# Layer 1 of a two-layer graph attention kernel: transposes in two separate halves, each beside a held piece of the projection

## The chip, the cores and the metric

The kernel runs on one core of a Trainium2 chip. The metric is the time of one execution on the device in microseconds. Three runs of the kernel before gave 1902.05, 1904.1 and 1896.26; the median is 1902.05 us. The profile is of one further execution.

The engines are named as in the profile: PE is TensorE (PEld are its weight loads), DVE is VectorE, ACT is ScalarE, POOL is GpSimd, SP is SyncE, whose queue here only issues DMAs.

## The reference

`x` has 3327 rows of 1024 numbers, `adj` is a 3327 x 3327 matrix of zeros and ones with about 0.5% ones and a full diagonal. There are two layers, each a graph attention with a residual and a layer norm. Layer 0 has 8 heads of 128, layer 1 has one head of 1024 and a relu:

```
# layer 0
h = x @ W0; e = leaky_relu(alpha_src[:, None] + alpha_dst[None, :])   # per head
x1 = layer_norm(x + softmax(where(adj == 0, -inf, e)) @ h)
# layer 1
h = x1 @ W1; e = leaky_relu(h @ a1 + (h @ a2).T)
out = layer_norm(x1 + relu(softmax(where(adj > 0, e, -9e15)) @ h))
```

## The kernel before, in words

Rows are worked on in 26 tiles of 128. A first stage (to about 480 us) projects `x`, scans `adj` into lists of neighbours, and decides between a dense and a sparse way; these inputs take the sparse one, `sparse`, L743. It runs layer 0 over all tiles and then layer 1 over all tiles, both by the function `pipeline` (L1058). The order in which instructions are issued is written out by hand (L1101, a manual schedule): what Python calls first stands first in each engine's queue, and each engine takes its queue in that order.

In layer 1 the attention sum is formed on the rows before the projection: the kernel sums the rows of layer 0's output `y_d`, divides, and projects the sum by `W1` afterwards (`wt1`). One tile of the class `Target` (L960) goes through these methods:

- `prepare` (L966) transposes the row scores to R on PE (L969) and takes their exp on ACT into the PSUM bank `way` (L971); it makes the one-hot marks on DVE (L833, L837) and loads the tile's own rows of `y_d` on SP's queue (L976). It is called for tile t+1 in block 2 of tile t.
- `fetch` (L988) gathers neighbours' rows by indirect DMAs of POOL (L817), four for each of blocks 0 to 3 and one for block 4, into a ring of five buffers, one tile ahead.
- `weights` (L994) makes the attention weights `es` of one block on DVE (L1001, L1002, L1004), through `way`.
- `sums` (L1007) adds a block into three accumulators on PE (L1013). Blocks 0 to 3 use four groups of 32 columns at a time; block 4 uses the full width.
- `close` (L1018) divides the sums and adds the tile's own row, giving `z` (DVE L1021 to L1023, ACT L1027, DVE L1030).
- `finish` (L1035) is a generator of ten steps. Steps 1 and 2 each transpose half of `z` on PE into the one bank of tag T (L176) and empty it on ACT into `xT` (L179). Steps 3 to 6 are the projection's first half of columns, two of eight `k` a step (L1045), with the relu and residual of that half on DVE at the end (L1048); steps 7 to 10 are the second half.
- `settle` (L1053) is the layer norm of the result and the store to `out`: DVE L192 to L194, ACT's square root L195, then after a yield DVE L197 and L199 and the DMA L1056. It is put on the queue `ahead` when the tenth step is done.

`pipeline` runs a tile's five blocks. In block 0 it closes the tile before; after each block's sums it runs steps of finished tiles from a queue `work`, and one step of `ahead`. For layer 1 the numbers are one step ahead of block 0's sums and then 2, 2, 2, 2 and 1 after the blocks' sums. So tile t has in block 0 the last step of tile t-2's projection, then its sums, then both transposes of tile t-1; after sums 1 to 3 four `k` of the projection of t-1 each, and after sums 4 two more.

ACT has to load a table ahead of the square root and another ahead of the exp of R; both loads stand in its queue in every tile of layer 1.

PSUM has eight banks. `sparse` gives five to the accumulators (tag A), one to the projection and to layer 0's denominators (S), one to transposes (T), one to `way` (E). In layer 1 a tile takes three of tag A.

The buffers of tag `z` (three) hold `z` and the output `o` in turn; `ys` (three, by t mod 3) holds the tiles' own rows.

Of the kernel before, what the change touches and what calls it, by code (L numbers as in the profile page):

```python
# [19 lines left out]
P = 128  # L20
# [6 lines left out]
def kernel(  # L27
# [31 lines left out]
    NT = (N + P - 1) // P  # L59
# [11 lines left out]
    EB = 4  # L71
# [5 lines left out]
    CUTS = (0, 342, 684, D + 1)  # L77
# [79 lines left out]
    class Phase:  # L157
# [7 lines left out]
        def bank(self, tag, shape, name, dt=F32):  # L165
            return self.psum.tile(shape, dt, tag=tag, name=name, bufs=self.banks[tag])
# [286 lines left out]
    with ExitStack() as own, tc.manual_schedule():  # L453
        ph = Phase(own, "proj", {"A": 2, "S": 1, "T": 2})
        pool, bank = ph.pool, ph.bank
# [205 lines left out]
        for t in range(3, NT):  # L661
# [3 lines left out]
            if t == 12:  # L665
                n, own = NT - 1, pool.tile([P, NT], I32, bufs=1, name="own")
# [27 lines left out]
        tr = bank("T", [1, P], "trc")  # L694
# [46 lines left out]


    def sparse(own):  # L743
        ph = Phase(own, "sparse", {"A": 5, "S": 1, "T": 1, "E": 1})
        pool, bank, sbuf = ph.pool, ph.bank, ph.sbuf
        NS = 5
        srcs = [pool.tile([P, NG, HG], F32, bufs=1, name=f"src{n}") for n in range(NS)]
# [8 lines left out]
        way = bank("E", [P, HALF], "way")  # L756
# [24 lines left out]
        def score_weights():  # L781
            for n, a in enumerate((a1_src, a1_dst)):
                av = sbuf("z", [P, D], 3, "av")
                spread(av, a)
                for k in range(KT):
                    pr = sbuf("pr", [P, D], 1)
                    nc.vector.scalar_tensor_tensor(
                        pr, wt1[:, k, :], 1.0, av, op0=OP.mult, op1=OP.mult, accum_out=wc[:, n, k : k + 1]
                    )
                    if k % 3 == 2:  # L790
                        yield
                for g in range(2):
                    tr = bank("T", [P, 4, P], "tr")
                    for k in range(4):
                        nc.tensor.transpose(
                            tr[:, k, :], wc[:, n, 4 * g + k : 4 * g + k + 1].to_broadcast([P, P]), ident
                        )
                    nc.scalar.activation(wa[n][:, g * HALF : (g + 1) * HALF], tr.rearrange("p a b -> p (a b)"), AF.Copy)
                yield

        def run(work, steps=1):

            while work and steps:
                try:
                    next(work[0])
                    steps -= 1
                except StopIteration:
                    work.popleft()

        ahead = deque([score_weights()])  # L810
# [17 lines left out]
        def marks(t):  # L828

            m = NB - 1  # L830
            oh = sbuf("oh", [P, m * GT + P], 2)
            parts = oh[:, : m * GT].rearrange("p (b t) -> p b t", t=GT), oh[:, m * GT :]
            nc.vector.tensor_tensor(  # L833
                parts[0], io_t[:, :GT].unsqueeze(1).to_broadcast([P, m, GT]),
                tgt[:, t, :m].unsqueeze(2).to_broadcast([P, m, GT]), OP.is_equal,
            )
            nc.vector.tensor_scalar(parts[1], io_t, tgt[:, t, m:], None, op0=OP.is_equal)  # L837
            return parts

        class Layer0:  # L840
# [5 lines left out]
            def prepare(self):  # L846
                self.re = listed.pop(self.t)
                self.oh, self.oh2 = marks(self.t)
                self.y = ys[self.t % 3]
                load_rows(self.y[:, :D], x, self.t)  # L850
                self.h = sbuf("own", [P, HW0], 2)
                nc.sync.dma_start(self.h, h0_d[self.t * P : (self.t + 1) * P, :])
# [13 lines left out]
            def begin(self):  # L866
                self.acc = [bank("A", [P, 4, DH], "acc") for _ in range(2)]
# [92 lines left out]
        class Target:  # L960
# [4 lines left out]

            def prepare(self):  # L966
                t = self.t
                tr = bank("T", [P, P], "tr")
                nc.tensor.transpose(tr, r1.s[:, t, :].to_broadcast([P, P]), ident)  # L969
                self.r = way[:, (t % 2) * P : (t % 2 + 1) * P].rearrange("p (g t) -> p g t", g=NG)  # L970
                nc.scalar.activation(  # L971
                    self.r.rearrange("p g t -> p (g t)"), tr, AF.Exp, scale=1 - SLOPE
                )
                self.oh, self.oh2 = marks(t)
                self.res = ys[t % 3]
                nc.sync.dma_start(self.res, y_d[t * P : (t + 1) * P, :])  # L976
# [12 lines left out]
                self.src[b] = gather(y_d, HW, self.t, b)  # L989

            def begin(self):
                self.acc = [bank("A", [P, CUTS[1]], "acc1") for _ in range(3)]

            def weights(self, b):  # L994
                s = self.src[b]
# [59 lines left out]
                for r in pieces(self.t):  # L1055
                    nc.sync.dma_start(out[at(self.t, r), :], o[r])  # L1056

        def pipeline(kind, late, behind, get):  # L1058

            tiles = [kind(t) for t in range(NT)]
            work = deque()
            get(0)
            tiles[0].prepare()
            for b in range(EB + 1):
                tiles[0].fetch(b)
            tiles[0].weights(0)
            for t, tg in enumerate(tiles):  # L1070
                tg.begin()
                for b in range(EB + 1):
                    if b == 0 and t:
                        tiles[t - 1].close()
                        run(work, late)
                    if b == 0 and t + 1 < NT:
                        get(t + 1)
                    if b == 2 and t + 1 < NT:
                        tiles[t + 1].prepare()
                    if b == 0:  # L1080
                        tg.own()
                    if b < EB:
                        tg.weights(b + 1)
                    elif t + 1 < NT:
                        tiles[t + 1].weights(0)
                    tg.sums(b)
                    if t + 1 < NT:
                        tiles[t + 1].fetch(b)
                    run(work, behind[b])
                    if t or b:  # L1090
                        run(ahead)
                if t == 0 and late:
                    work.append(iter(range(1)))
                work.append(tg.finish())
            tiles[-1].close()
            run(work, late)
            run(ahead, -1)
            run(work, -1)
            run(ahead, -1)

        with tc.manual_schedule():  # L1101
            pipeline(Layer0, 0, (1, 1, 1, 1, 1), get_edges)
            pipeline(Target, 1, (2, 2, 2, 2, 1), lambda t: None)


    def by_pairs(own):
# [119 lines left out]
    with arm.Else():  # L1226
        with ExitStack() as own:
            sparse(own)
# [23 lines left out]
```

## Time and profile before

| | |
|---|---|
| median of three runs | 1902.05 us (1896.26 to 1904.1) |
| profiled execution | 1954.92 us, span 1953.2 us, mean granted clock 0.907 |
| PE busy | 1668.2 us, 85% of the span |
| DVE, ACT, POOL busy | 1151.9, 546.6, 1039.7 us |
| first stage, layer 0, layer 1 | to about 480 us, to about 1215 us, from about 1240 us |
| sums of layer 1 (L1013) on PE | 265.1 us |
| projection of layer 1 (L1045) on PE | 382.3 us, 832 matmuls of 603 ns |
| transposes of z (L176), of R (L969), from 1210 us on | 35.2 us, 7.2 us |
| gathers of layer 1 (L817) on POOL | 416 into the ring, 1002 ns each, and 26 for block 4 |

How to read the views: a group's line names engine, line, operation, output and inputs, then the number of instructions, their busy time, and the idle time of the engine ahead of them with what ended it. The view of waits has for each waiter and releaser the total, the number and the longest. The timeline has the start, the time covered, and in brackets the engine's idle time before. "issue" means that the profile shows nothing that was waited for. In the slices each digit is a fortieth of the span, in tenths.

### The profile page before, as it was taken

The page shows a single profiled execution, that of the slowest core. Times are in us where ns is not written, and L with a number is a line of the kernel's source. Part 1 is how long each engine was busy: PE and PEld are TensorE (multiplying, and loading weights), DVE is VectorE, ACT ScalarE, POOL GpSimd, SP SyncE. Part 2 cuts the span into 40 slices and gives each one's busy share as a digit, 9 for nine tenths or more (in the row PEclk, how much of TensorE's full clock was granted, in tenths as well). Part 3 has the DMA queues.
Part 4 walks back from the last instruction along what each step waited for, and adds up shares of the span by engine and source line. Part 5 has one row for each costly group of instructions (what it writes and reads, how often), then busy time and mean ns, then how long its engine had stood idle before and what let it go on. Part 6 is the DMA issues. An engine that isn't in the chain of part 4 may idle for free.

```text
span 1953.2 us, 36865 instructions
## 1 busy us (share of the span) xinstructions
PE 1668.2 (85%) x14091; PEld 915.1 (47%) x14091; DVE 1151.9 (59%) x3087; ACT 546.6 (28%) x1422; POOL 1039.7 (53%) x1391
## 2 busy tenths in 40 slices
PE   8799999997577787777877777479999999999997
PEld 5456555564444554544454445134444444444343
DVE  6699989985575566556665566134444444444442
ACT  5445554442122222222222222012122222222221
POOL 4322222211666666666666663566666666666650
PEclk9899999998677887879787887589999999999999
DMA  7556554311999999999999996899999999999980
GB/s 183 95 129 130 112 94 92 88 60 64 404 356 377 370 365 387 381 372 363 379 377 375 369 371 225 335 318 386 378 378 367 381 366 373 357 377 368 355 340 32
DMA packets 171063, 567.68 MB, mean 291 GB/s; under 512 B 27690, under 2 KB 34346, under 8 KB 170878
## 3 DMA queue, kind: packets, MB, share of 16 engines
q0 software_dynamic: 131056, 455.68, 67.3%
q1 hardware_dynamic: 39822, 109.56, 15.1%
q8 instruction: 113, 1.85, 0.4%
q14 instruction: 72, 0.59, 0.1%
HBM read 578.85 MB, written 42.97 MB: 318 GB/s over the span
## 4 chain that ended last, share of the span: by engine, by line
PE 74%; issue 10%; DVE 6%; ACT 5%; DMA 2%; another core or an unknown queue 1%; POOL 1%; SPq 0%; POOLq 0%; DVEq 0%; ACTq 0%
PE mm L1045 19%; PE acc L914 19%; PE acc L1013 13%; PE mm L479 12%; PE acc L906 4%; PE acc L896 3%; ACT junk L311 3%; PE tr L176 2%; DMA wt<-in_L_gnn_W_dram 1%; DMA src<-h_d,idx 1%; PE den L922 1%; PE xp L411 1%; DVE top L274 1%; PE den L935 1%
## 5 line engine op out<-in xcount | busy, mean ns | idle before, releaser
L817 POOL DMA_INDIRECT src<-h_d,idx x416 | 448.9, 1079 | 228.0 <-PE acc L914 83.1
L817 POOL DMA_INDIRECT src<-y_d,idx x416 | 416.8, 1002 | 250.9 <-issue 84.4
L914 PE MATMUL acc<-src,e 128*32 128x128 f32 x6656 | 396.2, 321 | 167.0 <-issue 138.1
L914 PEld LDWEIGHTS acc<-src,e 128*32 128x32 f32 x6656 | 254.1, 127 | 332.5 <-issue 309.4
L479 PE MATMUL mm<-wt,xT 128*128 128x347 f32 (+1 forms) x1248 | 402.0, 468 | 3.0 <-DMA wt<-in_L_gnn_W_dram 2.6
L1045 PE MATMUL mm<-wt,xT 128*128 128x512 f32 x832 | 382.3, 603 | 3.1 <-DVE o L1048 3.1
L479 PEld LDWEIGHTS mm<-wt,xT 128*128 128x128 f32 x1248 | 228.2, 192 | 105.5 <-issue 4.0
L1013 PE MATMUL acc<-src,es 128*32 128x342 f32 (+1 forms) x2496 | 215.9, 467 | 39.2 <-DVE es L1004 24.9
L1045 PEld LDWEIGHTS mm<-wt,xT 128*128 128x128 f32 x832 | 151.9, 190 | 201.6 <-issue 184.9
L884 DVE TENSOR_TENSOR e<-oh,way 128x1024 f32<-128x1024 f32 x130 | 158.7, 1221 | 110.0 <-ACT w L882 29.5
L1013 PEld LDWEIGHTS acc<-src,es 128*32 128x32 f32 x2496 | 73.6, 112 | 171.5 <-issue 163.4
L882 ACT ACTIVATE w<-way 128x32 f32<-128x32 f32 x130 | 25.0, 193 | 449.1 <-PE acc L914 177.2
L1027 ACT ACTIVATE z<-y,ri 128x342 f32<-128x342 f32 (+1 forms) x78 | 39.5, 569 | 290.5 <-issue 118.7
L1001 DVE TENSOR_TENSOR way<-way,src 128x128 f32<-128x128 f32 x104 | 31.1, 299 | 147.2 <-ACT way L971 57.1
L1048 DVE SCALAR_TENSOR_TENSOR o<-mm,y 128x512 f32<-128x512 f32 x52 | 35.9, 691 | 108.9 <-PE mm L1045 73.9
L179 ACT ACTIVATE xT<-tr 128x512 f32<-128x512 f32 x104 | 59.4, 596 | 128.0 <-PE tr L176 115.0
L906 PE MATMUL acc<-own,ident 128*128 128x512 f32 x104 | 81.0, 871 | 0.0
L311 ACT ACTIVATE junk<-ad 128x3328 uint8<-128x3328 uint8 x26 | 78.4, 3014 | 2.5 <-POOL ad L308 2.5
L1021 DVE TENSOR_TENSOR ri<-acc,es 128x1 f32<-128x1 f32 x26 | 4.1, 158 | 124.3 <-PE acc L1013 116.7
L938 DVE TENSOR_TENSOR ri<-den,es 128x8 f32<-128x8 f32 x26 | 4.3, 166 | 119.8 <-PE den L935 119.8
L296 POOL CAST mvs<-r 128x8 bf16<-128x8 f32 x26 | 6.1, 235 | 122.8 <-ACT r L295 122.8
L864 ACT ACTIVATE own<-own,es 128x128 f32<-128x128 f32 x208 | 63.6, 388 | 26.2 <-DVE es L861 16.0
(194 smaller groups left out, 2020.8 us busy)
## 6 DMA issues: line engine op xcount, KB each, us to landing
h_d<-ht SPq DMA_DIRECT2D x26, 520.0 KB
own<-h_d SPq DMA_DIRECT2D x26, 520.0 KB
y_d<-y SPq DMA_DIRECT2D x26, 514.0 KB
y<-y_d SPq DMA_DIRECT2D x26, 514.0 KB
x<-in_x_dram SPq DMA_DIRECT2D x25, 512.0 KB
y<-in_x_dram SPq DMA_DIRECT2D x25, 512.0 KB
out_dram<-o SPq DMA_DIRECT2D x25, 512.0 KB
ad<-in_adj_dram POOLq DMA_DIRECT2D x25, 415.9 KB
```

The lines of the kernel that those rows point to most:

```text
L179: nc.scalar.activation(part, tr, AF.Copy)
L311: nc.scalar.activation(junk, ad, AF.Copy, accum_out=self.deg)
L479: nc.tensor.matmul(acc, xT[t][:, k, :], wt[:, k, CUTS0[c] : CUTS0[c + 1]], start=k == 0, stop=k == KT - 1)
L817: nc.gpsimd.indirect_dma_start(out=s[:, g, :w], out_offset=None, in_=table[:, :], in_offset=bass.IndirectOffsetOnAxis(ap=idx[:, t, b * NG ...
L864: nc.scalar.activation(hn, hn, AF.Copy, scale=es[:, n : n + 1])
L884: nc.vector.tensor_tensor(e, oh.unsqueeze(2).to_broadcast([P, ng, H, wide]), wp.unsqueeze(3).to_broadcast([P, ng, H, wide]), OP.mult,)
L896: nc.tensor.matmul(self.acc[h // 4][:, h % 4, :], e[:, 0, h, :], rowsof[:, 0, h, :], start=False, stop=h % 4 == 3,)
L906: nc.tensor.matmul(self.acc[b - 1].rearrange("p h d -> p (h d)"), ident, self.h[:, (b - 1) * HALF : b * HALF], start=False, stop=False,)
L914: nc.tensor.matmul(self.acc[h // 4][g * GT : (g + 1) * GT, h % 4, :], e[:, g, h, :], rowsof[:, g, h, :], start=first and h % 4 == 0, stop= ...
L1013: nc.tensor.matmul(self.acc[c][to, :m], es[:, g, :], s[:, g, CUTS[c] : CUTS[c + 1]], start=b == 0, stop=b == EB,)
L1027: nc.scalar.activation(z[:, cut], self.res[:, cut], AF.Copy, scale=ri[:, 1:2])
L1045: nc.tensor.matmul(acc, xT[:, k, :], wt1[:, k, half], start=k == 0, stop=k == KT - 1)
```

## The change

The generators of finished tiles are kept in a list `left` in place of the queue `work`, and a plan says for each of six places in a tile (ahead of block 0's sums, and after the sums of each of five blocks) which earlier tile runs a step: 2 is the tile two back, 1 the one before. In layer 1 the places are (2), (2, 1), (2, 1), (1, 1), (1, 1), (1). So the three places from the start of a tile each run one step (two `k`) of the projection of tile t-2; behind the second and the third of these follows one half of the transposes of tile t-1. The first half of its projection follows after sums 2 and 3, and one step of the second half after sums 4. Tile t-2's result is thus complete after sums 1, and its `settle` starts there. Layer 0's plan gives it the steps that it had: one of the tile before after each block's sums.

R's transpose writes the last quarter of the bank `way`, no longer the bank of tag T. Of the eight banks, tag A has four and S has two. `begin` takes the accumulators in the order 2, 0, 1, in which the sums use them.

```diff
-        ph = Phase(own, "sparse", {"A": 5, "S": 1, "T": 1, "E": 1})
+        ph = Phase(own, "sparse", {"A": 4, "S": 2, "T": 1, "E": 1})
...
-                tr = bank("T", [P, P], "tr")
+                tr = way[:, 3 * P :]
...
-                self.acc = [bank("A", [P, CUTS[1]], "acc1") for _ in range(3)]
+                self.acc = {c: bank("A", [P, CUTS[1]], "acc1") for c in (2, 0, 1)}
...
-        def pipeline(kind, late, behind, get):
-            tiles = [kind(t) for t in range(NT)]
-            work = deque()
+        def pipeline(tiles, plan, get):
+            left = []
+
+            def rest(t, n):
+                for who in plan[n]:
+                    k = t - who
+                    if 0 <= k < len(left):
+                        next(left[k], None)
+
...
                     if b == 0 and t:
                         tiles[t - 1].close()
-                        run(work, late)
+                        rest(t, 0)
...
                     tg.sums(b)
                     if t + 1 < NT:
                         tiles[t + 1].fetch(b)
-                    run(work, behind[b])
+                    rest(t, b + 1)
                     if t or b:
                         run(ahead)
-                if t == 0 and late:
-                    work.append(iter(range(1)))
-                work.append(tg.finish())
+                left.append(tg.finish())
             tiles[-1].close()
-            run(work, late)
+            for t in (NT, NT + 1):
+                for n in range(EB + 2):
+                    rest(t, n)
+                    run(ahead)
             run(ahead, -1)
-            run(work, -1)
-            run(ahead, -1)
...
-            pipeline(Layer0, 0, (1, 1, 1, 1, 1), get_edges)
-            pipeline(Target, 1, (2, 2, 2, 2, 1), lambda t: None)
+            pipeline([Layer0(t) for t in range(NT)], ((),) + ((1,),) * 5, get_edges)
+            pipeline(
+                [Target(t) for t in range(NT)], ((2,), (2, 1), (2, 1), (1, 1), (1, 1), (1,)), lambda t: None
+            )
```

## The prediction

> **What bounds the kernel now.** I first read the page in slices of 48.8 us, then the waits of TensorE from 1210 us to the end (layer 1), then one tile of layer 1 in order of time, then the busy times of that tile as a window.
>
> ```profile
> PE   8799999997577787777877777479999999999997
> ...
> PEclk9899999998677887879787887589999999999999
> DMA  7556554311999999999999996899999999999980
> ```
>
> Layer 1 fills the last 14 or so slices. There TensorE is at 9 and its granted clock is full, so this stage is TensorE's; the DMA engines are at 9 too and have to be looked at. The waits (who waited for whom: total us, times, longest):
>
> ```profile
> PE acc L1013 <- DVE es L1004: 24.9, 1, 24.9
> PE acc L1013 <- issue: 14.3, 12, 5.5
> PE tr L176 <- issue: 12.7, 18, 1.0
> PE tr L176 <- ACT xT L179: 11.7, 9, 2.8
> PE mm L1045 <- DVE o L1048: 3.1, 2, 2.3
> ```
>
> The 24.9 us is the start of the layer, once. The one idle time that returns in every tile stands before the transposes, L176: 12.7 + 11.7 = 24.4 us. The projection (L1045) waits 3.1 us in all, so its one bank costs almost nothing. In order of time (start, duration, engine, line, idle before):
>
> ```profile
> 1591.04 1.93 PE L1013 MATMUL acc<-src,es 128*32 128x341 f32 x24
> 1592.46 0.69 DVE L1048 SCALAR_TENSOR_TENSOR o<-mm,y 128x512 f32<-128x512 f32 x1 [1.54 <-PE acc L1013]
> 1592.90 0.66 PE L176 MATMUL tr<-ident,z 128*128 128x128 f32 x4
> ...
> 1593.60 0.60 ACT L179 ACTIVATE xT<-tr 128x512 f32<-128x512 f32 x1 [3.25 <-PE tr L176]
> ...
> 1594.25 0.66 PE L176 MATMUL tr<-ident,z 128*128 128x128 f32 x4 [0.69 <-issue]
> ...
> 1594.83 1.93 PE L1013 MATMUL acc<-src,es 128*32 128x341 f32 x24
> ...
> 1595.56 1.28 ACT L195 ACT_TABLE_LOAD   x1
> ...
> 1596.69 3.70 PE L1045 MATMUL mm<-wt,xT 128*128 128x512 f32 x8
> ...
> 1597.14 1.28 ACT L971 ACT_TABLE_LOAD   x1
> ...
> 1600.23 0.27 PE L969 MATMUL tr<-ident,sd 128*128 128x128 f32 x1
> 1600.43 1.93 PE L1013 MATMUL acc<-src,es 128*32 128x341 f32 x24
> ...
> 1603.23 0.26 ACT L971 ACTIVATE way<-tr 128x128 f32<-128x128 f32 x1 [4.81 <-PE acc L1013]
> 1603.52 0.30 DVE L1001 TENSOR_TENSOR way<-way,src 128x128 f32<-128x128 f32 x1 [4.62 <-ACT way L971]
> ```
>
> The second four transposes start 1.35 us after the first four: they want the same bank, which ScalarE empties in 0.60. From 1592.90 to 1594.83 the eight take 1.93 us. Next tile starts at 1616.58, so a tile is 25.54 us.
>
> **The skill.** "PSUM — Partial Sum Buffer", PSUM bank collisions, says to guard by bank, not by address; the trace agrees: DVE's L1001 waits for ScalarE's L971, which writes other columns of the bank `way`. "ScalarE: Activation LUTs", What ACT_TABLE_LOAD costs, gives 1283 ns a load, as here (1.28), but a drain behind it that this trace doesn't show: at 1595.56 + 1.28 = 1596.84 the square root follows at 1596.85. "Perfetto Trace Analysis", Tensor Engine Instruction, says that TensorE's end is an estimate and that its semaphore goes out later, after PSUM has acknowledged. That bears on L971, which starts 3.0 us after the matmul L969 that it needs, though ScalarE was free.
>
> **The change, part by part.**
>
> 1. *Halves apart.* An unhindered transpose takes 0.107 us (four loads in 0.42), a half 0.43. Today: first half to second half 1.35 plus 0.58 to the next sums = 1.93. After: half one stands behind two held k of the projection and before sums 1, half two likewise before sums 2. Each k is two matmuls of 0.427; eight of them between sums take 3.63 (8 x 0.427 + 0.21 for the change of shape), so two k take 4 x 0.427 + 0.21 = 1.92. Between sums 0 and sums 2 there stand today 1.93 + 3.74 (four k and R's transpose) = 5.67; after, (1.92 + 0.43) + (1.92 + 0.43 + 0.11) = 4.81. Gain 0.86 us a tile; the other pieces (four k, four k, two and two) keep their lengths. For tiles 2 to 25: 24 x 0.86 = 20.6. The drain at the end has one such wait more: 0.9.
>
> 2. *Held steps.* In tile 1 seven steps run in place of nine; two steps, 8 x 0.427 = 3.4 us, move to the drain. TensorE waits for gathers in tiles 0 and 1, so they were free there and are paid at the end: between 0 and 3.4 us lost, I take 3.4.
>
> 3. *Output clamp (L1048) and settle of tile t-2 one block later.* This is where the danger lies. After sums 1 come: clamp, statistics, square root (ScalarE), and behind that square root in ScalarE's queue R's exp (L971), behind which DVE's weights of block 3 wait for the bank. Counted from sums 0: sums 1 ends 6.12; the last held matmul starts at 6.12 + 1.39 and ends 0.6 later, 8.11. Clamp to 8.84, two statistics 1.27, aggregate 0.21, add 0.15, with gaps 10.58; ScalarE has emptied half two (9.24) and loaded its table (10.54), square root to 10.81, second load to 12.18, exp to 12.46, three weight operations (1603.52 to 1604.55: 1.03) to 13.5. Sums 3 wants them at 8.66 + 1.86 + 3.63 = 14.15. Hidden, with 0.6 us to spare; without that cover every us late costs a us a tile, 24 in all.
>
> 4. *SP queue.* The load of y for tile t+1 (L976) now waits for that clamp, and `out` of t-2 stands behind it. Out goes at about 14.6 in place of 7.1; it landed 6.5 to 8.2 us after issue, so by 21.1 to 22.8. z of this tile reuses that buffer at 22.4 and has 1.7 us to spare before the sums need it. Hidden. The y load lands about 9 us after issue, 18, and is wanted at 25.
>
> 5. *R's transpose in `way`.* It now waits for DVE's weights of block 2, done by about 2.6: nothing. *A 4, S 2.* With the new order the first accumulator of a tile has its bank two tiles back; the second and third need the first and second results of the close, done before the sums start. Bound for this: 0 to a gain of 3.1 (all waits of L1045); I take 0. Layer 0 keeps its order of steps; its second `den` bank removes waits that sum to 0.7 us or less: 0.
>
> Sum: -20.6 - 0.9 + 3.4 = -18 us. The profiled execution took 1954.92 with a span of 1953.2; the median is 1902.05, 2.8% less. Layer 1 runs at full clock in the profile, so I subtract the same 18 us from the median: 1884.
>
> **Does the DMA allow it?** Window of a tile, and the start of layer 0, where gathers are the bound (the last three columns: granted clock, DMA share, GB/s):
>
> ```profile
> 500.00:540.00 40.00, 23.24 (x314) 17.72 (x314) 23.91 (x45) 5.78 (x21) 25.05 (x23) 0.76 1.03 410
> 1591.04:1616.58 25.54, 24.85 (x144) 10.66 (x144) 10.90 (x32) 5.84 (x10) 16.99 (x17) 1.00 1.00 380
> ```
>
> Layer 1 moved 185.16 MB in 500 us, 9.46 MB a tile; in 24.68 us that is 383 GB/s of the 410 seen. POOL issues 17 gathers, one each 1.29 us: 21.9 us. Both fit, with 7 and 11% to spare.
>
> **Rivals.**
>
> *Slower: the signal from TensorE is late (chance 0.34).* L971 started 0.3 to 4.4 us after L969 had begun, in half of the tiles about 3.0, in steps of 1.4; its earliest was 0.31, so the lag is often 2.7. The delays build up while POOL issues gathers and clear when it pauses. Today nobody waits for R. After the change the clamp stands at the same place in the tile, at the head of the chain of part 3. Over 0.6 us late TensorE stalls at sums 3; over 0.6 + 0.86 = 1.5 us the tile is longer than before. At 2.7 the stall is 2.1, net 1.24 x 24 = 30, plus 3.4 less 0.9: about 1934. Against it: at 1606.04 the clamp of the other half followed its matmul within 0.1 us, and the profile itself runs 2.8% longer, so the lag may belong to profiling; the trace can't say.
>
> *Same (0.16).* Transfers or a part of that stall take what the transposes give: the DMA share is 1.00 already, which speaks for it; 410 GB/s speaks against. 1900.
>
> *The change doesn't do what it says:* the bank of `way` or the table loads put the wait of the transposes elsewhere. It is the same sum as the first two and lies in them.
>
> **From cases to numbers.** Forecast 0.50: 1884, its own range 1876 to 1892 (no end cost 1880; R's chain slipping by 0.3 us a tile 1891; first tiles some us better 1876). 0.5% of 1902 is 9.5 us, about what a measurement can tell: 1892.5 and 1911.5. The range reaches from 1876 to 1936 to take in the late signal; about 0.06 lies below, 0.13 above.
>
> **What would show it.** Right: L176's idle time falls from 24 to under 3 us, the two halves stand apart, a tile takes 24.7 us, sums 3 starts without a wait for DVE's es. Wrong: waits of L1013 for es L1004 in most tiles, L971 behind a late square root, or waits for gathers; then the tile is 25.5 us or more. A y load or z waiting for `out` would show part 4 wrong.

## The result, and the profile after

| | before | after |
|---|---|---|
| median | 1901.19 us (1896.26 to 1904.1) | 1876.69 us (1873.88 to 1880.8) |
| ratio, 95% interval | | 0.9878 (0.9862 to 0.9895) |
| profiled execution | 1954.92 us, span 1953.2 us | 1873.88 us, span 1872.2 us |
| a tile of layer 1 | 25.54 us | 24.68 us |

The change makes the kernel 24.5 us faster (20.0 to 26.2 by the interval); the forecast was 18. One thing is needed to read all that follows. The runs were on several chips of one type. On two of them the kernel before took 1895 to 1909 us (30 runs), on two others 1941 to 1964 us (62 runs); the result above is of the first kind. The profiled execution of before, by its time, was of the second kind, that of after of the first. So the two profiles are not compared by their spans. A kernel with the old order, profiled on a chip of the first kind (1895.5 us of span, told below), stands in for before.

The slices of the page after:

```profile
PE   8799999999366666666666765389999999999998
...
PEclk9899999999678888888878878699999999999999
DMA  7666555421799999999999999699999999999990
```

Layer 1 now shows 9 in every slice of TensorE up to the last, as before, and the DMA engines stand at 9 as before. A window over 24 and more tiles of layer 1 (start to end, length, busy time of PE, PEld, DVE, ACT, POOL, then granted clock, DMA share, GB/s):

```profile
1250.00:1870.00 620.00, 614.00 (x3488) 266.62 (x3487) 274.28 (x809) 141.67 (x245) 399.19 (x398) 1.00 0.94 364
```

TensorE is busy for 614 of 620 us: what can still be gained in this stage lies in its work, not in its waits. The waits of TensorE from 1150 us to the end (waiter, releaser, total us, times, longest):

```profile
PE acc L1013 <- DVE es L1004: 27.6, 3, 24.6
PE den L935 <- DVE met L934: 11.3, 2, 10.1
PE way L969 <- DVE es L1004: 5.6, 2, 3.2
PE acc L1013 <- DVE ri L1021: 2.6, 1, 2.6
...
PE acc L1013 <- DVE z L1030: 1.0, 1, 1.0
```

L176, which waited for 24.4 us in all before, is gone from the list. L1013 waits three times for weights, nearly all of it once, at the start of the layer. One tile in order of time (start, duration, engine, line, idle before); weight loads and GpSimd's gathers are left out of all such extracts, other gaps are marked:

```profile
1255.51 1.98 PE L1045 MATMUL mm<-wt,xT 128*128 128x512 f32 x4
1257.33 0.60 PE L176 MATMUL tr<-ident,z 128*128 128x128 f32 x4
1257.86 1.93 PE L1013 MATMUL acc<-src,es 128*32 128x341 f32 x24
...
1259.72 1.98 PE L1045 MATMUL mm<-wt,xT 128*128 128x512 f32 x4
1261.54 0.60 PE L176 MATMUL tr<-ident,z 128*128 128x128 f32 x4
1261.74 0.69 DVE L1048 SCALAR_TENSOR_TENSOR o<-mm,y 128x512 f32<-128x512 f32 x1 [2.70 <-PE mm L1045]
...
1262.18 0.60 ACT L179 ACTIVATE xT<-tr 128x512 f32<-128x512 f32 x1 [3.62 <-PE tr L176]
...
1264.09 0.20 ACT L195 ACTIVATE sg<-sg 128x1 f32<-128x1 f32 x1
...
1265.61 0.26 ACT L971 ACTIVATE way<-way 128x128 f32<-128x128 f32 x1
1265.90 0.30 DVE L1001 TENSOR_TENSOR way<-way,src 128x128 f32<-128x128 f32 x1 [1.04 <-ACT way L971]
...
1266.57 0.29 DVE L1004 TENSOR_TENSOR es<-way,oh 128x128 f32<-128x128 f32 x1
...
1267.67 1.93 PE L1013 MATMUL acc<-src,es 128*32 128x341 f32 x24
```

Each half stands behind a held piece of the projection and has no idle time in brackets. The chain that the forecast feared is all here: clamp at 1261.74, square root at 1264.09, R's exp at 1265.61, weights of block 3 done at 1266.57 + 0.29 = 1266.86. Sums 3 starts at 1267.67. Spare: 0.81 us, and it is the same in tile after tile.

### The profile page after: what moved, and what is told of

Read it like the earlier page. It is cut to its first block, busy times and chain, and to the rows that moved or that the text cites. A ratio compares the mean times of both kernels' runs of the same rounds, so it can differ in the third digit from the quotient of the medians.

```text
span 1872.2 us, 36820 instructions
## 1 busy us (share of the span) xinstructions
PE 1544.7 (83%) x14091; PEld 899.6 (48%) x14091; DVE 1146.3 (61%) x3087; ACT 546.5 (29%) x1422; POOL 1032.9 (55%) x1391
## 3 DMA queue, kind: packets, MB, share of 16 engines
q8 instruction: 113, 1.85, 0.4%
## 4 chain that ended last, share of the span: by engine, by line
PE 55%; DMA 21%; DVE 10%; ACT 6%; issue 5%; POOL 2%; DVEq 0%; SPq 0%; POOLq 0%; ACTq 0%
PE mm L1045 20%; DMA src<-h_d,idx 18%; PE mm L479 13%; PE acc L1013 12%; PE acc L914 5%; DVE e L884 3%; ACT junk L311 3%; POOL src L817 2%; PE tr L176 2%; DMA src<-y_d,idx 2%; DMA wt<-in_L_gnn_W_dram 1%; DVE pr L951 1%; PE acc L906 1%; PE xp L411 1%; ACT own L864 1%
## 5 line engine op out<-in xcount | busy, mean ns | idle before, releaser
L817 POOL DMA_INDIRECT src<-h_d,idx x416 | 441.3, 1061 | 205.5 <-PE acc L914 68.2
L1045 PE MATMUL mm<-wt,xT 128*128 128x512 f32 x832 | 387.6, 604 | 0.0
L914 PE MATMUL acc<-src,e 128*32 128x128 f32 x6656 | 268.3, 329 | 125.0 <-DVE e L884 125.0
L914 PEld LDWEIGHTS acc<-src,e 128*32 128x32 f32 x6656 | 228.6, 134 | 197.9 <-DVE e L884 118.1
L1045 PEld LDWEIGHTS mm<-wt,xT 128*128 128x128 f32 x832 | 149.7, 189 | 198.6 <-issue 193.6
L1013 PE MATMUL acc<-src,es 128*32 128x342 f32 (+1 forms) x2496 | 206.7, 464 | 31.2 <-DVE es L1004 27.6
L1013 PEld LDWEIGHTS acc<-src,es 128*32 128x32 f32 x2496 | 71.8, 111 | 148.3 <-issue 97.0
L179 ACT ACTIVATE xT<-tr 128x512 f32<-128x512 f32 x104 | 59.4, 596 | 250.2 <-PE tr L176 250.2
L935 PE MATMUL den<-heads,met 32*128 32x8 f32 x52 | 13.3, 326 | 111.8 <-DVE met L934 111.8
L879 DVE TENSOR_TENSOR way<-src,re 128x32 f32<-128x32 f32 x104 | 21.1, 203 | 133.0 <-DMA src<-h_d,idx 104.7
```

What stands on the lines that cost most here:

```text
L179: nc.scalar.activation(part, tr, AF.Copy)
L817: nc.gpsimd.indirect_dma_start(out=s[:, g, :w], out_offset=None, in_=table[:, :], in_offset=bass.IndirectOffsetOnAxis(ap=idx[:, t, b * NG ...
L914: nc.tensor.matmul(self.acc[h // 4][g * GT : (g + 1) * GT, h % 4, :], e[:, g, h, :], rowsof[:, g, h, :], start=first and h % 4 == 0, stop= ...
L1013: nc.tensor.matmul(self.acc[c][to, :m], es[:, g, :], s[:, g, CUTS[c] : CUTS[c + 1]], start=b == 0, stop=b == EB,)
L1045: nc.tensor.matmul(acc, xT[:, k, :], wt1[:, k, half], start=k == 0, stop=k == KT - 1)
```

## Experiments where the kernel before takes about 1900 us

**The old order with the new banks.** R's transpose stays in `way`, the banks stay at 4 and 2, and only the order goes back.

```diff
-((2,), (2, 1), (2, 1), (1, 1), (1, 1), (1,))
+((2,), (1, 1), (1, 1), (1, 1), (1, 1), (1,))
```

> The changed kernel with the steps of layer 1 in the order of before: one step ahead of block 0's sums, both halves of the transposes behind block 0's sums, then two steps behind each of sums 1 to 3 and one behind sums 4. What is left of the change is R's transpose in the bank of the weights and the split of the banks. A tile is 25.54 us again. Where the kernel before takes about 1901 us: if the deferral of two held steps from tile 1 to the drain costs the 3.4 us that the forecast took, the order alone is worth 20.6 + 0.9 - 3.4 = 18.1 and this run takes 1895, so that banks and R's transpose bring the other 6 us; if the deferral costs nothing, the order is worth 21.5 and this run takes 1898.5, 3 us less than before. The stretch from the last sums of layer 0 to the first block 4 of layer 1, and the drain behind the last block 4, show it beside the same stretches of the changed kernel: a loss of 3.4 shows as a drain that much longer after the 0.9 is taken off. Where the kernel before takes about 1950 us: about the ratio of banks and order of accumulators alone, 0.998; R's transpose without the bank of the halves then brings nothing of its own.

Measured: 1900.9 us, ratio 1.0004 (0.9992 to 1.0016). Banks and R's transpose alone bring nothing here; the order, put on top of them, brings the gain. Whether it would without them was not run on this kind of chip, nor were the order's moves run apart there; the traces have to part them. Of the two branches the one with 1898.5 is nearer, but it puts the saving in the wrong place, as the traces show. The waits of this kernel from 1150 us on:

```profile
PE tr L176 <- ACT xT L179: 19.9, 26, 2.8
```

That is 0.69 us in each of 25 tiles and longer only at the end. To find the rest I took from both traces the start of each tile's block 4 and laid the two spans side by side:

| stretch | old order | after | difference |
|---|---|---|---|
| start to block 4 of tile 0 | 1222.67 | 1222.50 | -0.17 |
| to block 4 of tile 1 | 28.90 | 25.89 | -3.01 |
| to block 4 of tile 25: 24 tiles | 612.86 | 592.24 | -20.62 |
| to the end | 31.08 | 31.53 | +0.45 |
| span | 1895.5 | 1872.2 | -23.35 |

Of the 20.62 us in 24 tiles, 16.5 are TensorE's idle time, which is gone; for the other 4.1 us its work itself has become shorter (596.4 us in the old order, 592.2 after).

Tile 1 is 3 us shorter. It is the tile that two held steps left, and the forecast held them to be free there. In the old order TensorE works through tile 1 like this:

```profile
1232.72 1.11 PE L176 MATMUL tr<-ident,z 128*128 128x128 f32 x4 [0.69 <-ACT xT L179]
1233.76 3.24 PE L1013 MATMUL acc<-src,es 128*32 128x341 f32 x24
...
1236.93 3.70 PE L1045 MATMUL mm<-wt,xT 128*128 128x512 f32 x8
...
1240.47 0.27 PE L969 MATMUL way<-ident,sd 128*128 128x128 f32 x1
1240.67 1.93 PE L1013 MATMUL acc<-src,es 128*32 128x341 f32 x24
```

and after the change:

```profile
1232.32 1.93 PE L1013 MATMUL acc<-src,es 128*32 128x341 f32 x24
...
1234.19 0.66 PE L176 MATMUL tr<-ident,z 128*128 128x128 f32 x4
...
1237.25 0.32 PE L969 MATMUL way<-ident,sd 128*128 128x128 f32 x1 [2.40 <-DVE es L1004]
1237.50 1.93 PE L1013 MATMUL acc<-src,es 128*32 128x341 f32 x24
```

The eight matmuls of L1045 in front of sums 2 are gone. A wait of 2.40 us takes part of their place, but sums 2 still starts 3.17 us earlier. In the old order the gathers were not what held tile 1. Part of the difference is the clock's: in the old order the granted clock is 0.5 from 1229.64 to 1236.46, after the change only from 1228.83 to 1232.24, so sums 1 takes 3.24 us there and 1.93 here. That is 1.3 of the 3.17 us, seen in one profile of each; that the order brings it is not shown.

The drain holds the second surprise. In the old order it has this:

```profile
1869.59 0.60 PE L176 MATMUL tr<-ident,z 128*128 128x128 f32 x4
...
1872.20 0.20 ACT L195 ACTIVATE sg<-sg 128x1 f32<-128x1 f32 x1 [4.89 <-DVE sg L194]
1872.31 0.58 ACT L179 ACTIVATE xT<-tr 128x512 f32<-128x512 f32 x1
...
1872.94 0.66 PE L176 MATMUL tr<-ident,z 128*128 128x128 f32 x4 [2.75 <-ACT xT L179]
1873.43 1.88 PE L1045 MATMUL mm<-wt,xT 128*128 128x512 f32 x4
```

The emptying of the first half (L179) stands in ScalarE's queue behind the square root of another tile (L195), which waits for VectorE's statistics. The bank therefore comes free 2.75 us late and not 0.69. From the start of the last tile's first transpose to the start of its projection the old order takes 3.84 us; after the change the two halves take 2 x 0.437 = 0.87. That saves 2.97 us and pays for most of the 3.43 us of projection (eight matmuls) that now lie in the drain: 3.43 - 2.97 = 0.46, as against the 0.45 measured.

**More cover ahead of sums 3.** Six `k` behind block 2's sums and two behind block 3's.

```diff
-((2,), (2, 1), (2, 1), (1, 1), (1, 1), (1,))
+((2,), (2, 1), (2, 1), (1, 1, 1), (1,), (1,))
```

> The changed kernel with six k of the projection behind block 2's sums and two behind block 3's, in place of four and four. The chain that ends in block 3's weights gets 4 x 0.427 = 1.7 us more room (0.81 + 1.71 = 2.5 us), and unlike the merged plan the clamp of the first half stays behind block 4's weights in DVE's queue. Theory (the late signal costs only where the chain to sums 3 has no room): where the kernel before takes about 1901 us nothing changes, 24.68 us a tile and 1877 us. Where it takes about 1950 us the wait of 2.66 us at sums 3 falls to about 1.0, 24 x 1.7 = 40 us less than the changed kernel's 1978, about 1938 to 1945, and block 4's sums no longer wait as in the merged plan. Rival (the merged plan gained by something else than the cover of sums 3, or its gain is spent at block 4 whatever stands there): no less than the merged plan's ratio of 0.998.

Measured: 1877.09 us, ratio 0.9881 (0.9862 to 0.9901), no different from after. The tile is 24.68 us, and the weights of block 3 are done 2.5 us ahead of their sums:

```profile
1266.31 0.29 DVE L1004 TENSOR_TENSOR es<-way,oh 128x128 f32<-128x128 f32 x1
...
1269.14 1.93 PE L1013 MATMUL acc<-src,es 128*32 128x341 f32 x24
```

So here the chain has room of 0.81 us or 2.5 us, and more room buys nothing.

**R's exp ahead of the square root.** `prepare` is split, and its first part is issued behind block 1's sums.

```diff
+                    if kind and b == 1 and t + 1 < NT:
+                        tiles[t + 1].score()
                     rest(t, b + 1)
```

> The changed kernel, but R's transpose and exp are issued directly behind block 1's sums, so ahead of the held step, of the second half's transposes and of the square root in ScalarE's queue. Block 3's weights then wait for VectorE's clamp and statistics alone and no longer for square root, second table load and exp (about 3 us of the chain). Theory (the square root in ScalarE's queue ahead of R's exp is what makes the chain long): where the kernel before takes about 1901 us no change, 1877 plus or minus 3; where it takes about 1950 us the wait at sums 3 falls from 2.66 to about 0.4 us, 24 x 2.2 = 53 us less than 1978, about 1925. Rival (the late clamp and the late signals alone set sums 3, whatever ScalarE's queue holds): no change there, about 1978.

Measured: 1878.69 us, ratio 0.9876 (0.9854 to 0.9898), no change, as both theories say for this kind of chip. Lines behind the split are moved by three in this kernel's timeline (its L1007 is L1004 of after):

```profile
1289.76 0.32 PE L969 MATMUL way<-ident,sd 128*128 128x128 f32 x1
...
1290.17 0.26 ACT L971 ACTIVATE way<-way 128x128 f32<-128x128 f32 x1 [1.52 <-PE way L969]
...
1295.52 0.29 DVE L1007 TENSOR_TENSOR es<-way,oh 128x128 f32<-128x128 f32 x1
...
1297.66 1.93 PE L1016 MATMUL acc<-src,es 128*32 128x341 f32 x24
```

Two readings. R's exp starts 0.4 us after R's transpose, in every tile from the third on: on this kind of chip TensorE's signals are on time. And the weights are done at 1295.81, 1.85 us ahead of sums 3; the square root in ScalarE's queue was worth about 1 us of the chain and not the 3 expected, for VectorE's own queue (clamp, statistics, marks) comes next.

**Both edits together.**

> Both edits of the two runs beside this: R's exp ahead of the square root, and six k behind block 2's sums and two behind block 3's. Theory: block 3's sums wait for nothing on either kind of chip. Where the kernel before takes about 1901 us: 1877. Where it takes about 1950: the changed kernel's 1978 less the whole wait of 2.66 us in 24 tiles (64 us), about 1914, ratio 0.982. Rival (something else than sums 3 is next: gathers of layer 1, or the second half's transposes waiting): the two edits do not add up, and the time stays at that of the better one alone.

Measured: 1880.72 us, ratio 0.9887 (0.9869 to 0.9905): again no change that the interval can tell from after. What these three would bring where the signals are late was not seen, since none of them ran on such a chip.

## Experiments where the kernel before takes about 1950 us

**The kernel before again**, unchanged, to see whether the late signal is that of one execution.

> The kernel before, unchanged, for a second profile. In the first one TensorE's signals reached other engines up to 4.4 us late; in the profile of the changed kernel none did. If that lag belonged to the one profiled execution, a tile of layer 1 takes 25.54 us here too, R's exp starts within 0.4 us of its transpose, the wait inside the transposes is 0.87 us in each of 25 tiles (some 22 us), and the span is near 1900 us. If the lag belongs to the kernel before, it is here again, with a span near 1953 us. It also gives the length of the first two tiles and of the drain, to compare with the changed kernel: the forecast has the changed one lose 3.4 us there, less 0.9.

Measured: 1948.29 us, where 43 runs of before had a median of 1949.73. The lateness is there again, as in the second branch, but it is neither the profiler's nor the kernel's own: the runs that are only timed take as long here, and 1900 us elsewhere. R's exp started more than 1 us after its transpose in 19 of 24 tiles (median 3.0), as in the first profile. It goes with the chip. Each of the four chips was used at one time only, so that the level would stay with a chip for good is not shown.

**Banks and the order of accumulators alone**, on the kernel before.

```diff
-        ph = Phase(own, "sparse", {"A": 5, "S": 1, "T": 1, "E": 1})
+        ph = Phase(own, "sparse", {"A": 4, "S": 2, "T": 1, "E": 1})
...
-                self.acc = [bank("A", [P, CUTS[1]], "acc1") for _ in range(3)]
+                self.acc = {c: bank("A", [P, CUTS[1]], "acc1") for c in (2, 0, 1)}
```

> The kernel before with the eight banks dealt as after (A 4, S 2) and the accumulators taken in the order 2, 0, 1, and nothing else. My theory: the banks alone bring 0 to 3 us (1898 to 1901), since the projection waited 3.1 us for its bank in all. Rival: the second bank of tag S or the order of the accumulators is what the gain comes from: 1877 to 1885.

Measured: 1945.29 us, ratio 0.9976 (0.9962 to 0.999), 4.7 us (1.9 to 7.4) less. Where signals are late, banks and order of accumulators are worth a little; where they are on time the old order above found nothing.

**Held pieces, but both halves together** ahead of block 1's sums.

```diff
-((2,), (2, 1), (2, 1), (1, 1), (1, 1), (1,))
+((2,), (2, 1, 1), (2,), (1, 1), (1, 1), (1,))
```

> The changed kernel with both halves of the transposes together again, after sums 0 and one held step; held steps, settle and banks stay as in the changed kernel. My theory: the second half waits for the bank again, 0.87 us a tile, 24 tiles: 21 us more than the changed kernel, 1895 to 1900. Rival: the gain comes from the held steps elsewhere, and the halves' place is worth little: within 5 us of 1877.

Measured: 1958.84 us, ratio 1.0043 (1.0026 to 1.006). Neither branch holds: theory had 21 us more than the changed kernel, and on the other chip of this kind the changed kernel takes 1978.5 us (below), 20 more than this one. The clamp of tile t-2 stands where the change puts it, and only the second half's transposes and their emptying are one block earlier. Two of the waits of TensorE from 1250 to 1900 us:

```profile
PE tr L176 <- ACT xT L179: 16.3, 22, 1.9
...
PE acc L1013 <- DVE es L1004: 4.0, 2, 2.0
```

The wait between the halves is back, as theory said, and sums 3 hardly waits (these two times), which theory did not think of.

**The change with R's transpose in the bank of the halves.**

```diff
-                tr = way[:, 3 * P :]
+                tr = bank("T", [P, P], "tr")
```

> The changed kernel with R's transpose back in the bank of tag T. It follows the second half of z's transposes at once, so it waits for ScalarE to empty that bank: in the changed kernel's trace R starts at 1261.98 and the bank is empty at 1262.78, so about 0.9 us a tile, 22 us in all: about 1898. The move into the bank of the weights is then a needed part of the change. Rival: the wait is hidden, or R's place is indifferent: 1877.

Measured: 2031.54 us, ratio 1.0419 (1.0379 to 1.0459). The waits of TensorE from 1250 to 1900 us:

```profile
PE tr L969 <- issue: 43.8, 13, 4.3
PE tr L969 <- DMA src<-y_d,idx: 24.8, 7, 4.3
```

R's transpose comes right behind the second half and wants the bank that ScalarE has yet to empty: 68.6 us in 20 waits, 3.4 us each. The view names other releasers, but in each of 24 tiles R's transpose starts 0.05 us after the emptying ends. This is far above the 0.69 us that the same hand-over costs where signals are on time, and above the 0.9 us a tile that was expected. So in the new order, on this kind of chip, R's own place is part of what makes it pay, though in the old order on the other kind it brings nothing.

**The changed kernel itself on such a chip.**

> The changed kernel once more, on the chip of these runs. The last four runs were on a chip on which the kernel before takes 1950 us in place of 1901 and TensorE's signals reach other engines late, by steps of 1.4 us, without the profile's causing it. If this is a chip of 1901: again 1877, 24 us faster. If it is a chip of 1950: my theory of the late signal says that the clamp and with it R's exp come late and TensorE stalls at sums 3, so the gain of 21 us is spent: from 10 us faster to 30 us slower than before there. Rival: the chain keeps its 0.8 us to spare or the lag falls elsewhere, and the change brings 20 us on such a chip too.

Measured: 1978.54 us (1969.51 to 1997.01), ratio 1.0171 (1.0119 to 1.0223): here the change makes the kernel *slower* by 29 us by the medians, 23 to 43 by the interval. The waits of TensorE from 1250 to 1850 us, then one tile:

```profile
PE acc L1013 <- DVE es L1004: 34.6, 18, 2.7
PE acc L1013 <- issue: 11.4, 13, 2.4
```

```profile
1568.81 0.60 PE L176 MATMUL tr<-ident,z 128*128 128x128 f32 x4
...
1570.22 0.69 DVE L1048 SCALAR_TENSOR_TENSOR o<-mm,y 128x512 f32<-128x512 f32 x1 [6.24 <-PE acc L1013]
...
1573.07 0.60 ACT L179 ACTIVATE xT<-tr 128x512 f32<-128x512 f32 x1 [7.24 <-PE mm L1045]
...
1574.98 0.20 ACT L195 ACTIVATE sg<-sg 128x1 f32<-128x1 f32 x1
...
1576.50 0.26 ACT L971 ACTIVATE way<-way 128x128 f32<-128x128 f32 x1
...
1577.80 1.93 PE L1013 MATMUL acc<-src,es 128*32 128x341 f32 x24 [2.66 <-DVE es L1004]
```

Set this beside the tile above. There the second half was emptied 0.64 us after its transposes had begun (1261.54, 1262.18); here 4.26 us after (1568.81, 1573.07), though ScalarE had been idle for 7.24 us. The signal itself is late: the trace has an update of the semaphore that ScalarE waits for at 1573.05, 0.02 us ahead of the emptying, and in the tile above at 1262.16, also 0.02 us ahead. Counted from the start of the last of a half's four transposes, the emptying starts at most 0.44 us later in the profile of after, and here more than 1 us later in 23 of 52 halves, 22 of them second halves. It stands ahead of the square root and R's exp in ScalarE's queue, so the whole chain slips, and sums 3 waits for 2.66 us; from the third tile on it waits in 21 tiles, 44.7 us in all. The clamp is late too, 1.84 us after its last matmul began in place of 0.63, but VectorE had its statistics ready at 1572.53 while the square root's table load began only at 1573.69, behind the emptying. So in this tile the emptying is the late link. The run with both halves together fits but does not decide it: there the emptying is on time (0.46 us at most, but for the layer's first), and so is the clamp at the head of the chain (0.63 us in 24 of 26 tiles).

**One and four idle copies ahead of R's exp.** ScalarE copies 128x512 of the weights `wt1` once, or four times, into a buffer that nobody reads; an emptying of that size takes 0.60 us. The edit for one copy:

```diff
+                idle = sbuf("idle", [P, HALF], 1)
+                nc.scalar.activation(idle[:, :512], wt1[:, 0, :512], AF.Copy)
```

> The changed kernel with one more ScalarE copy of 128 x 512 (0.6 us) just ahead of R's exp, whose result nobody uses. In the changed kernel's trace the weights of block 3 are ready 0.81 us before sums 3 want them (1266.86 against 1267.67). My theory: 0.6 us is hidden: within 3 us of the changed kernel. Rival (the chain is already what TensorE waits for, or the trace overstates the spare time): 0.6 us a tile, 15 us more.

> The changed kernel with four such copies ahead of R's exp, 2.0 us with their overlap (0.51 each after the first). My theory: 2.0 to 2.4 us less 0.81 to spare are paid in each of 24 tiles: 28 to 38 us more than the changed kernel, so slower than the kernel before; it shows what the chain costs when it is late. Rival: hidden elsewhere (another block's work fills in): under 10 us more.

Measured: 1997.64 us (ratio 1.0251, 1.0211 to 1.0291) and 2062.59 us (1.0585, 1.0551 to 1.0619). Against the changed kernel on the same chip that is 19 and 84 us more. For one copy the rival's 15 is the nearer number: on this chip the chain has no spare time. For four neither holds (28 to 38, or under 10). The traces show why it is so much. From block 4 of tile 1 to that of the last tile TensorE waits 46.8 us in the changed kernel, 56.3 with one copy and 103.8 with four, so four copies add 57 us of waits, 2.4 us in each of 24 tiles, which is 4 x 0.60. But the same matmuls also take longer, 602.4, 613.3 and 631.0 us, and the granted clock in this stretch is 0.989, 0.969 and 0.937. Of the 85.6 us that four copies add here, 28.6 thus go with the lower clock; of the 20.4 us of one copy, 10.9.

**Eight `k` behind block 2's sums and none behind block 3's.**

```diff
-((2,), (2, 1), (2, 1), (1, 1), (1, 1), (1,))
+((2,), (2, 1), (2, 1), (1, 1, 1, 1), (), (1,))
```

> The changed kernel with the projection's first half, eight k in one place after sums 2 and none after sums 3. If each change between the sums' shape and the projection's costs 0.21 us, one place fewer saves 0.2 us a tile: 5 us less than the changed kernel. Rival: back-to-back sums need the same drain, or block 4's weights, made later by DVE, are now late: no gain, or some us more.

Measured: 1945.83 us, ratio 0.9981 (0.9961 to 1.0001), 33 us less than the changed kernel there, where the branches had 5 us less or nothing. The waits of TensorE from 1250 to 1850 us:

```profile
PE acc L1013 <- issue: 27.5, 22, 8.7
PE acc L1013 <- DVE way L1002: 7.2, 8, 1.8
PE acc L1013 <- DVE es L1004: 1.4, 2, 0.7
```

With 3.4 us more of work in front of sums 3, sums 3 waits in no tile from the third on, where it waited 44.7 us. What is left now stands at block 4, whose weights come behind the clamp of the first half on VectorE (21.1 us in 24 tiles). From block 4 of tile 1 to that of the last tile this order takes 29.0 us less than the changed kernel; 24.2 of these are waits. The other 4.8 us are shorter work: the granted clock is higher (0.993 against 0.989), and there is one change of shape fewer, worth 5 us by the expectation; the run does not part the two. So most of the loss on such chips is the missing cover of that one chain.

## Why the prediction was right, and where not

| step of the forecast | forecast, us | measured, us |
|---|---|---|
| 1, halves apart, 24 tiles | -20.6 | -20.62 |
| 1, the same wait in the drain | -0.9 | -2.97 |
| 2, held steps added to the drain | +3.4 | +3.43 |
| 2, tiles 0 and 1, which the held steps left | 0 (free there) | -3.18 |
| 3, the chain's spare time | 0.6 a tile | 0.81 a tile |
| sum | -18 | -23.35 (medians: -24.5) |

**Step 1 was right to the hundredth.** The forecast took it from durations of single instructions at a full clock, and those were the same on both kinds of chip: the tile is 25.54 us in the old order on both.

**Step 2 was the mis-sized term.** "TensorE waits for gathers in tiles 0 and 1, so they were free there" is wrong where the result was measured. The profile of before came from the other kind of chip. There block 4 of tile 1 came 35.9 us after that of tile 0, where the same order takes 28.9 us here. I read a wait that the slower chip had made. Of the 3 us that tile 1 lost, the wait between its halves (0.69) and the granted clock (1.3) have a share, so not all of it is the two steps'. The bounds that I gave, 0 to 3.4 lost, had this end in them: -20.6 - 0.9 alone gives 1880.5, and with the drain's 2.07 us more the sum reaches 1878.5.

**The drain's 0.9** was the wait of a steady tile carried to a place where another tile's square root stands ahead on ScalarE. It measured 2.97.

**Step 3 and the slower rival.** The chain has its links and its order as written, and 0.81 us to spare. Its sum had a small slip: by the lengths of step 1 sums 3 is due at 14.02 and not 14.15; it came at 14.03, and the chain ended at 13.22 in place of 13.5. The late signal decides, as the rival said, and it exists. Its price was put at 33 us with a stall of 2.1 us; where it occurs the stall reaches 2.7 us and the loss is 29 us. What the rival had wrong is whose it is. I left open whether it belonged to profiling. It goes with the chip: there every timed run of before takes about 1950 us, and on the others the profile shows no such delay. It also had the late signal at the clamp, while the later one is at the emptying of the second half. The forecast's subtraction from the median held because the layer 1 tile is the same on both kinds.

**Where luck came in.** Which of the two cases came true was decided by the chip on which the result was measured, and the forecast did not know that chips differ. Its profile came from the kind of chip on which the change loses. The number lies at the fast end of what was given for this case (1876 to 1892).

**Steps 4 and 5.** No wait for `out` or for the y load appears among TensorE's waits in layer 1, and from the third tile on transfers hold nothing up: the rival "same" did not occur. R's transpose in `way` costs nothing, as said. The banks are worth 0 here (ratio 1.0004) and 4.7 us on the slower chips, where the interval of 1.9 to 7.4 us does not exclude the 3.1 us that I gave as their bound.

**Open.** Why some chips deliver TensorE's signals late. The forecast saw the delays clear when GpSimd pauses, but such a pause can itself end with TensorE (at 1563.10, after 4.09 us, `<-PE acc L1013`), so the traces do not say which follows which. Open too is whether six and two `k`, R's exp first, or both would keep the gain there. From the merged plan, 1.7 us of cover ought to return most of a stall of 2.66; it is argued and not shown.

## What to carry to other kernels

Cut a pair of operations that share one bank and put other work of the same engine between them: the gain here was the hand-over's idle time and a little more (0.86 us a tile, 0.69 of it idle), and it could be summed from single durations. Then look at what the move puts at the head of a chain through in-order queues, and leave it cover for more than the spare time that one profile shows: 0.81 us was enough on one kind of chip, and on the other the same order cost 29 us. And when the profiled execution and the median differ by some per cent, ask first which waits of that profile exist in the runs that are timed, above all at the start and the end of a stage.

## What the runs showed of the hardware

- One program has two levels of time on chips of one type, 1900 and 1950 us, with the same granted clock (the medians of before's runs are 0.917 to 0.920 on all four chips). At the upper level, what follows TensorE starts late, in steps of about 1.4 us (0.31, 1.65, 3.03, 4.48 us for R's exp in the second profile of before); at the lower level, in the profile of after, no emptying starts more than 0.44 us late. The Trainium skill, "Perfetto Trace Analysis", Tensor Engine Instruction, says that the end of a matmul in the trace is an estimate and that the signal leaves only when PSUM has acknowledged; the traces agree that the two differ, and show that the difference is not a constant.
- Layer 0 is slower at the upper level as well: from its first to its last tile (L938) it takes 635.6 us in the profile of after and 669.0 and 665.1 in the two of before, some 30 of the 50 us. That late signals do this is not shown. From 480 to 1150 us the DMA share is about 1 in all of them, but the DMAs move 372 and 374 GB/s there and 391 in the profile of after.
- When TensorE waits more in layer 1, its granted clock falls, to 0.5 for 3.4 us at a time. From block 4 of tile 1 to that of the last tile the mean is 1.000 with 16.5 us of waits (the old order), 0.989 with 46.8 (the changed kernel on a slower chip), 0.956 with 77.6 (R's transpose in the bank of the halves) and 0.937 with 103.8 (four copies). No single wait of the changed kernel there is longer than 2.8 us.
- A switch of ScalarE's tables cost 1.28 us and no more: in the tile after the change the load for R's exp starts at 1264.31 and the exp at 1265.61, 0.02 us after its end. The Trainium skill, "ScalarE: Activation LUTs", What ACT_TABLE_LOAD costs, adds a drain of 1380 ns, which no run here shows.
